# A decoder's router by column tiles, parts shared by a lane's two sequences, and shared experts as threads of their own

## Chip, cores and metric

The kernel runs on one core of a Trainium2 chip. The metric is the time of one execution on the device in microseconds (us). The kernel before has a median of 859.11 us over 13 runs.

## What is computed

Two decoder layers run over x of 16 sequences of 128 tokens with 256 features, in float32. Layer 0 is causal attention with one head, attention to a context of the same size with 16 heads of 16, and a feed-forward part of 16 blocks of which a router keeps four for each token. Layer 1 is self-attention with 16 heads, windowed attention to the context with a rotary embedding, and eight experts of which a router picks two for each token, beside shared experts that all tokens pass. Every part works on the layer norm of x and is added to x:

```python
x = x + _L0_attn_ref(_layernorm(x), qk, ov)
x = x + _L0_xattn_ref(_layernorm(x), ctx, ctx, mask, ...)
x = x + _L0_ffn_ref(_layernorm(x), w_router, b_router, w1, b1, w2, b2)
x = x + _L1_attn_ref(_layernorm(x), w_qkv, b_qkv, w_o, b_o)
x = x + _L1_xattn_ref(_layernorm(x), ctx, ctx, cell, ...)
x = x + _L1_ffn_ref(_layernorm(x), gate_weight, w_gate, w_up, w_down, ws_gate, ws_up, ws_down)
```

The two routers are small products: 256 features to 16 block scores, and 256 features to 8 expert scores, for each token.

## The kernel before

**Lanes.** Eight lanes hold two sequences each (`G = 2`), so a lane is 256 tokens. Its x stays on the chip as `[128 tokens, 2, 256]`. Each part of a layer is a Python generator: it normalises x (`normalise`, line 390: VectorE's bn_stats and bn_aggr, four short GpSimd instructions for `rstd` and `less`, then the two sequences' `xn`, one on VectorE and one on ScalarE), transposes it on TensorE (`tps`, four transposes, copied by ScalarE into `srcT`), and multiplies.

**An attention** (`attention`, for 48 pairs of lane and sequence) takes two passes over the scores. TensorE makes s from `kb` and `qT` in row tiles of 32 (lines with `s<-kb,qT`), sixteen small products add the mask (`s<-unseen,ident`), VectorE takes the maxima (`top`), TensorE transposes them (`topT`), ScalarE and GpSimd put them into the queries (`less`, `qs`), TensorE makes s again (`s<-qs,kb`), ScalarE takes exponentials (`p`), and TensorE multiplies with the values in column tiles of 32 (`oT<-p,v`), transposes (`o`) and hands to VectorE. The score banks (`s`) are two, both taken by one attention at a time.

**Experts.** Lanes 0 to 4 are sorted: `routing` scatters their tokens to DRAM by expert (GpSimd's indirect DMAs), `plan` lays out 27 tiles of 128 rows, and `expert_tile` gathers a tile's weights and rows (`we`), transposes (`xgt`), multiplies (`gu<-we,xgT`), gates, transposes (`hT`), multiplies (`y<-we,hT`) and writes to `by_experts`. `combining` gathers the results back (`yg`, twenty gathers) and adds them to x. Lanes 5 to 7 run all eight experts densely (`expert_ffn`), with `wb` spreading each token's weight. Shared experts of a sorted lane run inside `routing`, as a second thread beside the choice, on the same `srcT`.

**The order of the work** is written when the kernel is built. `Turns` (line 82) is a planner: each generator yields the engine that it wants next and the tiles that it takes, and `run` always resumes the thread with the smallest key: the planned start, then "takes score banks" first, then rank. Costs are planner figures in ns; `SWITCH` is charged when TensorE's tile shape changes, `PART` when TensorE goes to another part, `LEAD` is how far a part that takes score banks may go ahead of its time. `LIMITS` says how many buffers of each kind there are. What the planner decides is then fixed: each engine carries out its own list in order, with semaphores between the engines. `more` starts lanes: five are in flight at once, in the order `TURN`.

**Lines that the steps touch.** `router` (668) makes 16 or 8 scores with the token chunk as the stationary operand and the router's weights moving, two products a sequence; `project` (461) and `values` (488) work one sequence at a time; `causal_attention` (724) runs one thread a sequence; the sums after the feed-forward parts (`y0`, `y1`) are made and added one sequence at a time; lines 134 and 139 are the planner's helpers through which all products and all transposes are recorded, 143 VectorE's, 147 ScalarE's, 153 GpSimd's, 166 the indirect DMAs, 172 and 187 the DMA loads and writes.

Of the kernel before, what the change touches and what calls it, by code (L numbers as in the profile page):

```python
# [54 lines left out]
    ("L1_xattn_b_q", 2), ("L1_xattn_b_k", 2),  # L55
# [3 lines left out]
    ("L1_xattn_b_v", D), ("L1_xattn_b_o", D), ("L0_ffn_b_router", NB),  # L59
# [22 lines left out]
class Turns:  # L82
# [6 lines left out]
    LEAD = 200.0  # L89
# [3 lines left out]
    PART = 40.0  # L93
# [22 lines left out]
    def give(self, tag, n=1):  # L116
        self.tiles[tag] += [self.now.at] * n
# [27 lines left out]
    def act(self, name, out, *args, **kw):  # L145
        self.charge(ACT, 200 + 0.8 * self.width(out, args))
        getattr(self.nc.scalar, name)(out, *args, **kw)  # L147
# [79 lines left out]
    def run(self, more):  # L227

        while True:
            more()  # L230
            best = None
            for i, th in enumerate(self.threads):
                if th.ask is None:
                    continue
                engine, takes = th.ask
                at = self.reach(th, engine)
                ok = True
                for tag, n in takes.items():
                    left = sorted(self.tiles[tag])
                    if not n:  # L240
                        continue
                    if len(left) < n:
                        ok = False
                        break
                    at = max(at, left[n - 1])
                first = "s" in takes
                key = (max(at - self.LEAD * first, self.free_at[engine] - first), not first, th.rank, i)
                if ok and (best is None or key < best[0]):
                    best = key, th, at
# [14 lines left out]
class Thread:  # L264
    def __init__(self, gen, rank, at, parent):
        self.gen, self.rank, self.at, self.parent = gen, rank, at, parent
        self.last, self.ask, self.waits, self.children, self.result = None, None, 0, [], None
# [3 lines left out]
def decoder(ctx: ExitStack, tc: tile.TileContext, a: dict, out: bass.AP):  # L271
# [83 lines left out]
    class Sorted:  # L355
# [3 lines left out]
        def __init__(self, k, lanes):  # L359
            self.lanes, self.left = lanes, len(lanes)  # L360
# [21 lines left out]
        bank=4, s=2, oT=1, xn=5, xT=4, qk=5, qs=2, kb=3, v=3, p=6, oS=2, on=4, xe=3, hm=5, tmp=4,  # L382
        rank=2, selT=2, p0=3, pT0=3, unseen=4, chosen=3, swap=1, words=1, top=3,
# [77 lines left out]
    def project(w, at, xT, j):  # L461

        q.landed(w)
        t = bank([P, D], "pr")
        for d in range(DC):
            q.matmul(t, xT[:, d, j * S : (j + 1) * S], w[:, d, at : at + D], start=d == 0, stop=d == DC - 1)
        return t

# [19 lines left out]
    def values(w, at, xT, bias):  # L488
        yield PE, dict(v=1, bank=1)
        v = v_tiles.pop(0)  # L490
        for j in range(G):
            if j:
                yield PE, dict(bank=1)
            t = project(w, at, xT, j)
            yield DVE
            q.dve(
                "tensor_tensor",
                v[:, j, 0 : H * HA].rearrange("p (h e) -> p h e", e=HA)[:, :, 0:HD],
                t.rearrange("p (h e) -> p h e", e=HD),
                row(bias).rearrange("p (h e) -> p h e", e=HD),  # L500
                ALU.add,
            )
            q.give("bank")
# [29 lines left out]
    def attention(qT, kb, v, j, unseen=None, to=None):  # L533
# [7 lines left out]
        yield PE, dict(s=2)  # L541
        ss = banks()
# [11 lines left out]
        for t2, s in enumerate(ss):  # L554
# [4 lines left out]
            q.give("s")  # L559
        yield PE, dict(bank=1)  # L560
# [16 lines left out]
        yield PE, dict(s=2)  # L577
        ss = banks()
# [12 lines left out]
        def exponentials(s):  # L591
# [3 lines left out]
            q.give("s")  # L595
            return p

        pTs = yield [exponentials(s) for s in ss]
        yield PE, dict(oT=1, bank=1)
# [18 lines left out]
        q.give("bank")  # L618
        yield PE, dict(bank=1)
# [48 lines left out]
    def router(w, xT, n):  # L668
        yield PE, dict(bank=1)
        t = bank([P, G, n], "rt")  # L670
        for j in range(G):
            for d in range(DC):
                q.matmul(t[:, j, :], xT[:, d, j * S : (j + 1) * S], w[:, d, :], start=d == 0, stop=d == DC - 1)
        return t

    def output_projection(on, w, l, j, gain=None, bias=None, free=None):
# [16 lines left out]
        y = project(w, 0, oT, 0)  # L693
# [30 lines left out]
    def causal_attention(l):  # L724
# [8 lines left out]
        def one(j):  # L733
            js = slice(j * S, (j + 1) * S)
            yield PE, dict(bank=1)
            t = project(w["ov"], 0, xT, j)
            yield ACT, dict(on=1)
            v = new("on", [P, D], "v1")
            q.act("copy", v, t)
            q.give("bank")  # L740
            yield PE, dict(bank=1)
            s = bank([P, S], "s0")
            for d in range(DC):
                q.matmul(s, qT[:, d, js], xT[:, d, js], start=d == 0, stop=d == DC - 1)
            yield DVE, dict(p0=1)
            p = new("p0", [P, S], "p0")
            q.dve("tensor_tensor", p, s, causal, ALU.add)
            q.give("bank")
            m = small.tile([P, 1], F32, tag="m0", name="m0")
            q.dve("tensor_reduce", m, p, AX.X, ALU.max, negate=True)  # L750
            yield ACT
            total = small.tile([P, 1], F32, tag="total", name="total")
            q.act("activation", p, p, AF.Exp, bias=m, accum_out=total)
            yield PE, dict(bank=1)
            t = bank([P, S], "pt0")
            q.transpose(t, p, ident)
            q.give("p0")
            yield ACT, dict(pT0=1)
            pT = new("pT0", [P, S], "pT0")
            q.act("copy", pT, t)  # L760
            q.give("bank")
            yield PE, dict(bank=1)
            o = bank([P, D], "o0")
            q.matmul(o, pT, v, start=True, stop=True)
            q.give("pT0")
            q.give("on")
            yield DVE
            r = small.tile([P, 1], F32, tag="r0", name="r0")
            q.dve("reciprocal", r, total)
            q.dve("scalar_tensor_tensor", x[l][:, j, :], o, r, x[l][:, j, :], ALU.mult, ALU.add)  # L770
            q.give("bank")

        yield [one(j) for j in range(G)]
        q.give("xT")
        q.give("qk")

# [32 lines left out]
    def block_ffn(l):  # L809

        xT = yield from transposed((yield from normalise(x[l])))
        rt = yield from router(w["r0"], xT, NB)
        yield DVE, dict(chosen=1)
        pr = small.tile([P, G, NB], F32, tag="pr", name="pr")
        q.dve("tensor_tensor", pr, rt, row("L0_ffn_b_router").unsqueeze(1).to_broadcast([P, G, NB]), ALU.add)
# [15 lines left out]
        for j in range(G):  # L831
            q.pool("tensor_tensor", x[l][:, j, :], x[l][:, j, :], row("L0_ffn_b2"), ALU.add)
# [21 lines left out]
        for j in range(G):  # L854
            yield PE, dict(bank=1)
            y = bank([P, D], "y0")
            for f in range(8):
                q.matmul(
                    y, hm[f // 2][:, f % 2, j * S : (j + 1) * S], w["w2"][:, f, :], start=f == 0, stop=f == 7
                )  # L860
            if j == G - 1:
                q.give("hm", 4)
            yield DVE
            q.dve("tensor_tensor", x[l][:, j, :], x[l][:, j, :], y, ALU.add)
            q.give("bank")

    def self_attention(l):
# [4 lines left out]
        def residual():  # L872
            for j in range(G):

                yield POOL
                q.pool("tensor_tensor", xn[:, j, :], xn[:, j, :], row("L1_attn_b_o"), ALU.add)
                q.pool("tensor_tensor", x[l][:, j, :], x[l][:, j, :], xn[:, j, :], ALU.add)
# [24 lines left out]
    def windowed_attention(l):  # L902
# [31 lines left out]
        def one(j):  # L934
            unseen = yield from by_rows(hidden[1][l * G + j])
            yield from attention(qT, kb, v, j, unseen=unseen, to=on[:, j, :])
            q.give("unseen")
            yield POOL
            q.pool("tensor_tensor", x[l][:, j, :], x[l][:, j, :], row("L1_xattn_b_o"), ALU.add)

        yield [one(j) for j in range(G)]
# [10 lines left out]
    def routing(l):  # L952
# [5 lines left out]
        def choice():  # L958
            rt = yield from router(w["r1"], xT, NE)
            yield ACT  # L960
            sc = small.tile([P, G, NE], F32, tag="sc", name="sc")
            q.act("activation", sc, rt, AF.Exp, scale=-1.0)
            q.give("bank")
# [42 lines left out]
        yield [choice(), shared(l, xT)]  # L1006
        q.give("xT")

    def shared(l, xT):
# [13 lines left out]
        for j in range(G):  # L1023
            yield PE, dict(bank=1)
            y = bank([P, D], "y1")
            for f in range(DC):
                q.matmul(y, hm[:, f, j * S : (j + 1) * S], w["shared"][:, f, 2 * D :], start=f == 0, stop=f == DC - 1)
            if j == G - 1:
                q.give("hm")
            yield DVE  # L1030
            q.dve("tensor_tensor", x[l][:, j, :], x[l][:, j, :], y, ALU.add)
            q.give("bank")
# [198 lines left out]
    def expert_ffn(l):  # L1231

        xT = yield from transposed((yield from normalise(x[l])))
        rt = yield from router(w["r1"], xT, NE)
        yield ACT
        sc = small.tile([P, G, NE], F32, tag="sc", name="sc")
        q.act("activation", sc, rt, AF.Exp, scale=-1.0)
        q.give("bank")
# [47 lines left out]
        for j in range(G):  # L1286
            yield PE, dict(bank=1)
            y = bank([P, D], "y1")
            for f in range(NE + DC):
                down = w["down"][:, f * D : (f + 1) * D] if f < NE else w["shared"][:, f - NE, 2 * D :]  # L1290
                q.matmul(
                    y, hm[f // 2][:, f % 2, j * S : (j + 1) * S], down, start=f == 0, stop=f == NE + DC - 1
                )
            if j == G - 1:
                q.give("hm", 5)
            yield DVE
# [232 lines left out]
```

## Time and profile before

| | us |
|---|---|
| median of 13 runs | 859.11 |
| lowest run | 857.28 |
| the profiled execution, its own time | 857.88 |
| its span, first to last instruction | 856.1 |

| engine | busy us | share of the span |
|---|---|---|
| TensorE, matmuls (PE) | 787.4 | 92% |
| TensorE, weight loads (PEld) | 617.6 | 72% |
| VectorE (DVE) | 471.1 | 55% |
| GpSimd (POOL) | 446.4 | 52% |
| ScalarE (ACT) | 386.5 | 45% |

A product in float32 stands in the trace as two records, a transpose or a bf16 product as one. In a line of the timeline the first number is the start, the second how long the merged records last, and a bracket gives how long the engine sat idle before it and who ended that. Records of TensorE overlap, so the pace of a run of products is read from start to start. PEclk is the clock that TensorE was granted, as a share of full speed.

### The profile page before, as it was taken

How to read it: one execution, taken by the hardware profiler on the slowest of the kernel's cores; microseconds unless marked ns; L12 is line 12 of the kernel's file. 1: busy time of each engine (PE TensorE's matmuls, PEld its weight loads, DVE VectorE, ACT ScalarE, POOL GpSimd, SP SyncE). 2: the span in 40 equal slices, each digit the busy share in tenths (PEclk: the TensorE clock that was granted, in tenths of full speed). 3: DMA queues.
4: the chain of work that ended last, by engine and by line, in shares of the span. 5: the costliest groups of instructions: out<-in, count | busy, mean ns of one | idle time of the engine just before them, and what ended most of it. 6: DMA issues, size and time to landing. Idle time of an engine off the chain costs nothing.

```text
span 856.1 us, 19669 instructions
## 1 busy us (share of the span) xinstructions
PE 787.4 (92%) x7866; PEld 617.6 (72%) x7866; DVE 471.1 (55%) x1232; ACT 386.5 (45%) x864; POOL 446.4 (52%) x700
## 2 busy tenths in 40 slices
PE   6999899999999999999999999899977897989948
PEld 5877578878877777778776777677655575867836
DVE  5535545546544642654767766775784553345534
ACT  4545445343436534364565756346363444343200
POOL 4333636214534534742768759856578654552350
PEclk9999899999999999999999999999998999999988
DMA  8365514410300001001402201001115342452231
GB/s 286 130 179 187 169 42 147 129 26 26 93 27 15 1 2 50 2 3 50 142 32 76 76 14 57 26 26 38 63 63 167 106 136 82 142 159 94 74 105 50
DMA packets 60939, 70.40 MB, mean 82 GB/s; under 512 B 8848, under 2 KB 52496, under 8 KB 60208
## 3 DMA queue, kind: packets, MB, share of 16 engines
q1 hardware_dynamic: 51584, 46.20, 17.0%
q0 software_dynamic: 5376, 19.40, 7.5%
q10 hardware_dynamic: 3888, 3.54, 1.2%
q8 instruction: 62, 1.02, 0.5%
q14 instruction: 29, 0.24, 0.1%
HBM read 43.96 MB, written 20.97 MB: 76 GB/s over the span
## 4 chain that ended last, share of the span: by engine, by line
PE 71%; DVE 9%; POOL 6%; ACT 5%; issue 4%; another core or an unknown queue 2%; DMA 1%; ACTq 0%; DVEq 0%; POOLq 0%
PE s L134 13%; PE y L134 11%; PE pj L134 10%; PE pr L134 9%; PE gu L134 9%; PE hp L134 7%; PE oT L134 4%; PE tps L139 3%; POOL rstd L153 2%; PE o L139 2%; ACT p L147 2%; PE rt L134 1%; DVE top L143 1%; DVE st L143 1%
## 5 line engine op out<-in xcount | busy, mean ns | idle before, releaser
L143 DVE TENSOR_REDUCE top<-s 128x8 f32<-128x1024 f32 x96 | 112.8, 1217 | 57.6 <-PE s L134 50.7
L147 ACT ACTIVATE p<-s 128x1024 f32<-128x1024 f32 x96 | 95.4, 1026 | 52.6 <-PE s L134 43.7
L153 POOL TENSOR_TENSOR qs<-qT,less 128x512 f32<-128x512 f32 x48 | 61.8, 1292 | 89.8 <-ACT less L147 79.8
L134 PE MATMUL hp<-srcT,L_w 128*128 128x256 f32 x256 | 65.9, 387 | 0.6 <-DVE v L143 0.5
L134 PE MATMUL s<-qs,kb 32*128 32x128 f32 x1536 | 59.6, 283 | 7.0 <-POOL qs L153 3.5
L134 PE MATMUL s<-kb,qT 32*128 32x256 f32 x768 | 63.7, 421 | 2.1 <-ACT p L147 2.0
L134 PEld LDWEIGHTS s<-qs,kb 32*128 32x128 f32 x1536 | 49.4, 186 | 21.7 <-issue 8.1
L153 POOL TENSOR_SCALAR rstd<-mv 128x2 f32<-128x2 f32 x72 | 16.5, 229 | 90.4 <-DVE mv L143 66.4
L147 ACT ACTIVATE sg<-gu 128x256 f32<-128x256 f32 (+1 forms) x67 | 22.6, 341 | 90.2 <-PE gu L134 66.7
L134 PE MATMUL gu<-srcT,gu 128*128 128x256 f32 x192 | 51.1, 416 | 9.4 <-DVE hm L143 6.1
L134 PE MATMUL y<-L_w,hm 128*128 128x256 f32 x256 | 58.5, 381 | 0.7 <-DVE x L143 0.7
L153 POOL TENSOR_TENSOR rstd<-rstd,power 128x2 f32<-128x2 f32 x72 | 51.9, 720 | 6.0
L134 PE MATMUL oT<-p,v 128*32 128x128 f32 x1536 | 53.6, 281 | 1.3 <-ACT p L147 1.3
L153 POOL TENSOR_SCALAR kb<-kT,consts 128x256 f32<-128x256 f32 x96 | 53.5, 570 | 1.8 <-ACT kT L147 0.8
L134 PEld LDWEIGHTS gu<-srcT,gu 128*128 128x128 f32 x192 | 38.1, 207 | 21.9 <-DVE hm L143 10.7
L134 PEld LDWEIGHTS y<-L_w,hm 128*128 128x128 f32 x256 | 47.8, 190 | 8.3 <-issue 1.3
L134 PEld LDWEIGHTS hp<-srcT,L_w 128*128 128x128 f32 x256 | 44.5, 190 | 12.1 <-issue 2.9
L134 PEld LDWEIGHTS s<-kb,qT 32*128 32x128 f32 x768 | 39.6, 193 | 18.6 <-issue 9.0
L147 ACT ACTIVATE less<-topT,consts 128x128 f32<-128x128 f32 x96 | 29.6, 372 | 47.1 <-PE topT L139 44.1
L147 ACT COPY oS<-oT 128x512 f32<-128x512 f32 x48 | 28.3, 589 | 46.4 <-PE oT L134 46.1
L134 PEld LDWEIGHTS oT<-p,v 128*32 128x32 f32 x1536 | 40.0, 112 | 12.5 <-issue 8.5
L166 POOL DMA_INDIRECT we<-in_L_experts,tile_weights x27 | 26.6, 984 | 41.6 <-ACT sg L147 14.6
(211 smaller groups left out, 1777.2 us busy)
## 6 DMA issues: line engine op xcount, KB each, us to landing
to_experts<-zero SPq DMA_DIRECT2D x7, 1280.0 KB
unseen<-hidden SPq DMA_DIRECT2D x128, 64.0 KB
c<-in_ctx SPq DMA_DIRECT2D x16, 256.0 KB
by_experts<-we ACTq DMA_DIRECT2D x27, 128.0 KB
x<-in_x SPq DMA_DIRECT2D x8, 256.0 KB
L_w<-in_L_w SPq DMA_DIRECT2D x2, 1024.0 KB
hidden<-plain SPq DMA_DIRECT2D x32, 64.0 KB
swap<-qT SPq DMA_DIRECT2D x16, 128.0 KB
```

What stands on the lines that cost most here:

```text
L134: self.nc.tensor.matmul(out, lhsT, rhs, **kw)
L139: self.nc.tensor.transpose(out, src, ident)
L143: getattr(self.nc.vector, name)(out, *args, **kw)
L147: getattr(self.nc.scalar, name)(out, *args, **kw)
L153: getattr(self.nc.gpsimd, name)(out, *args, **kw)
L166: self.nc.gpsimd.indirect_dma_start(out, at(out_index), src, at(src_index))
```

## The change

It touches the routers, several parts that had been made once for each sequence, the shared experts of the sorted lanes, and the planner.

1. **Router.** The weights are padded to 32 columns and become the stationary operand; four products (two sequences by two feature chunks) write four strips of 32 partitions of one bank `rT`. ScalarE copies it (with the bias of the block router), one transpose brings tokens back to the partitions, and VectorE's reduce adds the two chunks.
2. **A lane's two sequences share parts**: one bank and one copy for the values, one thread of the causal attention for both, one bank and one add for the feed-forward sums (`products`), and one GpSimd add in place of two for biases and residuals.
3. **Shared experts** of lanes 0 to 4 become threads of their own, started when routing ends; they normalise and transpose x again. `combining` starts when all of the group's lanes and the sorted tiles have ended (`part_ended`).
4. **Planner**: `LEAD` 200 to 100, `PART` 40 to 20, a tile given back counts as free 30 ns later (`RELEASE`), ScalarE's operands by row cost 80 ns each, a thread that holds score banks keeps the priority (`holds`), among equals a score or `oT` part goes first while TensorE is in a tiled shape (`tiled`); buffers qs 2 to 3, tmp 4 to 3, p0 and pT0 3 to 2; six lanes in flight in place of five, and layer 1 of lane 0 follows six lanes of layer 0 in place of seven.

```diff
-    LEAD = 200.0
+    LEAD = 100.0
...
-    PART = 40.0
+    PART = 20.0
+    RELEASE = 30.0
...
-        self.tiles[tag] += [self.now.at] * n
+        self.tiles[tag] += [self.now.at + self.RELEASE] * n
...
-                first = "s" in takes
-                key = (max(at - self.LEAD * first, self.free_at[engine] - first), not first, th.rank, i)
+                first = th.holds or "s" in takes
+                tiled = engine == PE and self.shape != WHOLE and ("s" in takes or "oT" in takes)
+                key = (max(at - self.LEAD * first, self.free_at[engine] - first), not first, not tiled, th.rank, i)
...
-        bank=4, s=2, oT=1, xn=5, xT=4, qk=5, qs=2, kb=3, v=3, p=6, oS=2, on=4, xe=3, hm=5, tmp=4,
-        rank=2, selT=2, p0=3, pT0=3, unseen=4, chosen=3, swap=1, words=1, top=3,
+        bank=4, s=2, oT=1, xn=5, xT=4, qk=5, qs=3, kb=3, v=3, p=6, oS=2, on=4, xe=3, hm=5, tmp=3,
+        rank=2, selT=2, p0=2, pT0=2, unseen=4, chosen=3, swap=1, words=1, top=3,
...
-    def router(w, xT, n):
+    def router(w, xT, n, bias=None):
         yield PE, dict(bank=1)
-        t = bank([P, G, n], "rt")
+        t = bank([P, S], "rT")
         for j in range(G):
             for d in range(DC):
-                q.matmul(t[:, j, :], xT[:, d, j * S : (j + 1) * S], w[:, d, :], start=d == 0, stop=d == DC - 1)
-        return t
+                c = j * DC + d
+                q.matmul(
+                    t[c * CT : (c + 1) * CT, :], w[:, d, :], xT[:, d, j * S : (j + 1) * S], start=True, stop=True
+                )
+        yield ACT, dict(p0=1)
+        sb = new("p0", [P, S], "rT")
+        if bias is None:
+            q.act("copy", sb, t)
+        else:
+            q.act("activation", sb, t, AF.Identity, bias=col(bias, 0))
+        q.give("bank")
+        yield PE, dict(bank=1)
+        t = bank([P, G * DC, CT], "rt")
+        q.transpose(t.rearrange("p c n -> p (c n)"), sb, ident)
+        q.give("p0")
+        return t.rearrange("p (g d) n -> p g n d", d=DC)[:, :, 0:n]
...
+    def products(parts):
+
+        y = bank([P, G, D], "y")
+        for j in range(G):
+            pairs = parts(slice(j * S, (j + 1) * S))
+            for i, (a, b) in enumerate(pairs):
+                q.matmul(y[:, j], a, b, start=i == 0, stop=i == len(pairs) - 1)
+        return y
...
-            q.dve("tensor_tensor", p, s, causal, ALU.add)
+        q.dve("tensor_tensor", p, s, causal.unsqueeze(1).to_broadcast([P, G, S]), ALU.add)
...
-        yield [one(j) for j in range(G)]
...
+        for j in range(G):
+            q.act("activation", p[:, j], p[:, j], AF.Exp, bias=m[:, j : j + 1], accum_out=total[:, j : j + 1])
...
-        yield [choice(), shared(l, xT)]
-        q.give("xT")
-
-    def shared(l, xT):
+        yield from choice()
+
+    def shared(l):
+
+        g = group_of[l]
+
+        xT = yield from transposed((yield from normalise(x[l])))
...
+        y = products(lambda js: [(hm[:, f, js], w["shared"][:, f, 2 * D :]) for f in range(DC)])
...
+        part_ended(g)
+
+    def part_ended(g):
+
+        g.parts -= 1
+        if g.parts == 0:
+            at = q.now.at
+            for l in g.lanes:
+                q.start(combining(g, l), 2 * NL + l, at)
...
             g.left -= 1
+            at = q.now.at
+            q.start(shared(l), 2 * NL + l, at)
             if g.left == 0:
-                q.start(sorted_experts(g), 2 * NL + min(g.lanes), q.now.at)
+                q.start(sorted_experts(g), 2 * NL + min(g.lanes), at)
...
-    IN_FLIGHT = 5
+    IN_FLIGHT = 6
...
-    TURN = [(0, l) for l in range(7)]
+    TURN = [(0, l) for l in range(6)]
     for l in range(NL):
-        TURN += [(1, l), (0, l + 7)] if l + 7 < NL else [(1, l)]
+        TURN += [(1, l), (0, l + 6)] if l + 6 < NL else [(1, l)]
```

## The prediction

> **What bounds the kernel now.** I read the page first, then busy time by stretches, then TensorE's timeline, the waits, and last the order in which the instructions of both programs stand on each engine.
>
> ```profile
> span 856.1 us, 19669 instructions
> ...
> PE 787.4 (92%) x7866; PEld 617.6 (72%) x7866; DVE 471.1 (55%) x1232; ACT 386.5 (45%) x864; POOL 446.4 (52%) x700
> ...
> PE   6999899999999999999999999899977897989948
> ...
> PEclk9999899999999999999999999999998999999988
> ```
>
> TensorE is busy 92% of the span and no other engine is over 55%: TensorE is the bound, so a part's cost counts by what it takes on TensorE, and the other engines by how long they leave it idle. The PE row has its low digits in the last quarter. The stretches (us; then busy us of PE, PEld, DVE, ACT, POOL with instructions; granted clock; DMA) put numbers on that:
>
> ```profile
> 8.00:50.00 42.00, 41.02 (x211) 35.14 (x211) 21.78 (x79) 22.38 (x60) 16.58 (x43) 1.00 0.63 209
> 50.00:100.00 50.00, 45.95 (x686) 33.02 (x687) 29.22 (x60) 23.77 (x51) 22.72 (x35) 0.94 0.60 185
> 100.00:640.00 540.00, 517.06 (x5773) 405.48 (x5774) 318.75 (x802) 269.79 (x560) 300.13 (x481) 1.00 0.16 50
> 640.00:806.00 166.00, 146.96 (x1056) 115.20 (x1055) 79.31 (x235) 65.03 (x184) 84.93 (x108) 0.94 0.38 117
> 806.00:834.00 28.00, 17.05 (x69) 13.26 (x68) 9.43 (x23) 2.09 (x6) 17.63 (x19) 0.88 0.41 119
> 834.00:856.00 22.00, 17.94 (x76) 14.76 (x76) 11.03 (x29) 1.54 (x4) 0.00 (x0) 0.90 0.14 48
> ```
>
> From 100 to 640 TensorE is idle 23 of 540 us at full clock: only less work on TensorE shortens it. From 640 on, where the expert tiles run beside the last lanes, it is idle 19.0 of 166 us and the clock is 0.94, so up to 10.0 us more go to the clock (0.06 x 166). From 806 the combining gathers and the last lane's experts leave 11.0 us idle in 28.
>
> **The sum** is made against the profiled execution (857.88 us, span 856.1); the median of the runs shown is 859.11, 1.2 above, which I add at the end. A measurement of this kernel tells about 0.2% (1.7 us) from no change.
>
> **1. Routers.** TensorE's timeline (start, us, then the instructions):
>
> ```profile
> 114.39 1.08 PE L134 MATMUL oT<-p,v 128*32 128x128 f32 x32
> 115.40 1.13 PE L134 MATMUL hp<-srcT,L_w 128*128 128x256 f32 x4
> ...
> 116.48 1.03 PE L134 MATMUL hp<-srcT,L_w 128*128 128x256 f32 x4
> ...
> 117.45 0.96 PE L134 MATMUL rt<-L_router,srcT 128*128 128x16 f32 x8
> 118.27 0.63 PE L139 MATMUL o<-consts,oS 128*128 128x128 f32 x4
> ```
>
> Read from start to start. The old router's 8 records hold TensorE from 117.45 to 118.27, 0.82 us. The new one has the shape of oT (128*32, 128 moving columns), whose 32 records take 1.01 us (114.39 to 115.40): 8 x 0.032 = 0.26 us. Its one transpose costs a quarter of four (0.44 us in rows like o's): 0.11. So 16 routers x (0.82 - 0.26 - 0.11) = -7.2 us. Changing the shape of the array costs 1.13 - 1.03 = 0.10 us; in the orders the changes between whole, row, column and small tiles go from 329 to 333, since the new picking rule sets most routers beside other tiled parts: +0.4 us. If the four column tiles did not run side by side, a router would cost 0.82 + 0.11 + 0.2. The transpose waits for ScalarE's copy (0.28 us, 0.46 with a bias); in the new order 0.4 to 11 us of TensorE's other parts stand between the two (15 of 16 have over 1 us), so behind it on TensorE nothing is held, and the scores come some 0.7 us later to VectorE.
>
> A rule speaks against this step: the Trainium skill, "TensorEngine Tiling (Array Packing)", Instruction Overhead, gives a matmul some 60 cycles however few columns move. By it (an estimate at that section's figure and the 2.4 GHz of "TensorE: Matmul & The Clock Gate") the old router would cost 8 x 0.025 = 0.2 us, and the swap would lose 2.7 us instead of winning 7.2. The row above, 0.10 us per record beside weight loads of 0.2 us mean, decides.
>
> **2. Shared experts as threads.** For five lanes x is normalised and transposed again: 20 transposes x 0.11 = +2.2 us of TensorE. The rest lies on idle engines: VectorE 5 x (2 x 0.407 + 2 x 0.182 + 0.479) = 8.3 us, GpSimd 5 x (0.229 + 0.720 + 0.204 + 0.252) = 7.0, ScalarE 5 x (0.605 + 0.590) = 6.0. GpSimd gets 49.2 us of 256-wide adds back as 32 instructions of 512 (nearest row 1.27 to 1.30 us): 41 us, so it ends 1 us lower. In the most loaded stretch it is 80% busy; without that cover the 7.0 would count. ScalarE also gets 16 router copies (0.28 to 0.46 us each), some 6 us on an engine idle over half the span.
>
> **3. Shared parts.** TensorE's work is the same. VectorE has 24 adds of 512 for 48 of 256 (0.417 each; 512 lies between 0.68, the rank compare, and 0.84, the rotation): between 0 and -3.6 us, hidden. Joined causal attention lengthens a lane's chain by (0.417 - 0.282) + (0.407 - 0.286) + 0.603 + 0.100 + 0.484 = 1.44 us. Other lanes cover it, except at the start: from nothing to 2 x 1.44 = 2.9 us. I take +0.7, because the nearest row, the wait before lane 0's first projection (8.61), is 0.68 and the stretch 8 to 50 has 0.98 idle in all. The last add is 512 wide and waits for both sequences: +0.4 at the end (0 to 0.42).
>
> Work on TensorE: -7.2 + 0.4 + 2.2 = **-4.6 us**; start and end +1.1.
>
> **4. The order.** Six lanes instead of five, LEAD 100, PART 20, RELEASE 30, kept priority for the s parts and qs = 3 cost no instruction; they move parts, and the SP queue carries the same 274 entries. Laid along the orders, the paces above (0.215 us a record of 256 columns, 0.11 a transpose, 1.08 for sixteen s<-kb, 1.10 for thirty-two s<-qs, 0.37 for sixteen masks, 1.02 for oT) add up to 726 us before and 721 after. On that scale the first gathered expert tile stands at 575 and 578, but the last attention's maximum transpose at 618 and 593, the last windowed output at 648 and 621, the last router at 660 and 656. So the last lane's chain from output to router gets 35 us of other work beside it instead of 12, and the five shared pairs move from 362-544 to 452-595. On GpSimd, between the first and the last tile gather, 66 other instructions became 36: two qs instead of four, 4 kb instead of 8, five normalisations instead of seven. What the old order pays there:
>
> ```profile
> 714.38 0.33 PE L139 MATMUL hT<-consts,h 128*128 128x128 f32 x1 [3.13 <-ACT oT L147]
> 715.08 3.63 PE L134 MATMUL pr<-L_xo,oT 128*128 128x256 f32 x8 [0.37 <-ACT oT L147]
> ...
> 766.06 0.29 PE L134 MATMUL ptt<-ident,chosen 128*128 128x128 bf16 x2 [2.87 <-DVE sc L143]
> 766.18 3.63 PE L134 MATMUL gu<-srcT,gu 128*128 128x256 f32 x8
> ```
>
> Each wait of about 3 us is followed by eight records at 3.63 us where they otherwise take 1.89: 1.74 more. With the waits for qs (1.4) and xn (1.4) these chains cost 3.1 + 2.9 + 2 x 1.74 + 2.8 = 12.2 us. The moved parts win between nothing and 12.2 (a new wait of that size in the middle would turn it to a loss, see rival A); half of the layer-1 parts left this stretch and the chain has thrice the cover, so I take two thirds: **-8 us**. Behind these waits gather issues on GpSimd (0.95 us every 1.25) and the by_experts writes on ScalarE's queue. Next late are the xgT copies (4.9 us of waits), which belong to the tiles and stay, as do the 11.0 us from 806 to 834: 20 gathers follow the last tile in both orders.
>
> The Trainium skill, "TensorE: Matmul & The Clock Gate", HAM oscillation, asks for no idle gaps over some 3.4 us. Here gaps of 3.1 and 2.9 us already halve the pace, so a smaller gap costs too; by the rule alone those 3.5 us would not be in the sum.
>
> 857.9 - 4.6 + 1.1 - 8 + 1.2 = 847.6: I forecast **847 us**.
>
> **Rivals.**
> A, slower: the pace of the expert tiles sets the tail. The 27 tiles go from their first row gather at 642.0 to the last tile's copy at 801, 5.9 us each, while a tile needs only 1.6 us of TensorE. If six row buffers, the gathers and the write back hold that pace, less work beside it wins nothing; tiles start 3 us later by the order, and start and end cost 1.1: 859.1 + 3 + 1.1 = 863. It decides once the tiles keep above 5.7 us. For it: GpSimd waits for buffers (14.6 us by sg, 7.9 by by_experts). Against: these are 33 of 166 us, and tiles are picked last, behind lanes that now leave earlier. Chance 0.18.
> B: the order wins nothing, the work alone counts: 859.1 - 4.6 + 1.1 = 855.6. For it: 100 to 640 has little to win. Chance 0.27.
> C, the column tiles run one after another: 16 x 0.31 + 2.2 + 1.1 = +8.3, 867. The oT row speaks against it. Chance 0.03.
> My forecast: 0.52, with 836 to 852 as its own range.
>
> Together: faster 0.52 + 0.22 of B, 0.74; within 0.2% 0.05 (of B); slower 0.21. The range runs from 835 (all 12.2 us won, and some of the 11 after 806) to 863 (rival A's time).
>
> **What would show it.** Right: new routers at 0.25 to 0.3 us from start to start, TensorE's clock from 640 on at 0.96 or more, fewer than 15 us idle in that stretch, no 3 us wait before an output projection or ptt. Wrong: idle from 100 to 640 above 30 us (six lanes crowd the tiles), tiles at 5.9 us each, or a stretch of the gathers longer than the old 28 us.

## The result and the profile after

The changed kernel takes 847.57 us (median of 7 runs, 845.68 to 850.42) where the kernel before takes 859.51 (31 runs): a ratio of 0.987, 95% interval 0.985 to 0.988. The profiled execution took 845.64 us against 857.88. The forecast said 847. The sum came out; half of its terms did not, and most of this part is about that.

The page of the changed kernel (span, busy time, the span in 40 slices, the granted clock):

```profile
span 843.9 us, 19702 instructions
...
PE 775.6 (92%) x7902; PEld 610.5 (72%) x7902; DVE 474.2 (56%) x1201; ACT 393.8 (47%) x874; POOL 446.7 (53%) x688
...
PE   6999999999999999999899899989894899989938
...
PEclk9999999999999999999999999989897899999969
```

TensorE's busy time fell by 11.8 us (787.4 to 775.6) and the rest of the span by 0.4 (68.7 to 68.3). So practically all of the gain is less busy time on TensorE, and the idle time that the forecast wanted to win is still there. The stretches of the changed kernel say where (us; busy us of PE, PEld, DVE, ACT, POOL; granted clock; DMA):

```profile
8.00:50.00 42.00, 41.33 (x242) 35.92 (x243) 21.66 (x72) 21.76 (x54) 17.58 (x46) 1.00 0.63 207
50.00:100.00 50.00, 49.63 (x754) 37.79 (x753) 31.59 (x61) 28.26 (x60) 24.82 (x42) 1.00 0.55 159
100.00:640.00 540.00, 517.03 (x5956) 404.85 (x5954) 324.45 (x781) 283.60 (x586) 309.01 (x474) 0.98 0.17 53
640.00:806.00 166.00, 143.21 (x855) 112.62 (x856) 79.23 (x245) 54.93 (x165) 86.65 (x106) 0.94 0.43 130
```

From 8 to 100 us TensorE was idle 5.0 us and is now idle 1.0. From 100 to 640 nothing changed (22.9 and 23.0). From 640 to 806 it is idle 22.8 us where it was 19.0, at the same clock of 0.94. The timeline of TensorE shows why; the bracket is the wait before the line:

```profile
637.85 0.42 PE L135 MATMUL rT<-srcT,L_router 128*32 128x128 f32 x8
641.17 0.68 PE L140 MATMUL o<-consts,oS 128*128 128x128 f32 x4 [2.90 <-DVE on L144]
641.64 0.42 PE L140 MATMUL rt<-consts,rT 128*128 128x128 f32 x1
647.94 1.38 PE L140 MATMUL ot<-consts,xn 128*128 128x128 f32 x4 [5.87 <-DVE xn L144]
649.14 3.31 PE L135 MATMUL pr<-L_xo,oT 128*128 128x256 f32 x8
...
753.34 0.28 PE L135 MATMUL ptt<-ident,chosen 128*128 128x128 bf16 x2 [2.34 <-DVE chosen L144]
753.46 5.36 PE L135 MATMUL gu<-srcT,gu 128*128 128x256 f32 x16
```

Of the two old waits that of 3.13 us is gone; the one before `ptt` is still there, 2.34 us where it was 2.87. New waits of 2.90 and 5.87 us stand in front of other transposes. The eight records of `pr` take 3.31 us where such a part takes 1.99 at full clock: the clock is at half from 641.6 on for 10.2 us.

### The profile page after: what moved, and what is told of

The parts are those of the page before. It is cut to its first block, busy times and chain, and to the rows that moved or that the text cites. A ratio compares the mean times of both kernels' runs of the same rounds, so it can differ in the third digit from the quotient of the medians.

```text
span 843.9 us, 19702 instructions
## 1 busy us (share of the span) xinstructions
PE 775.6 (92%) x7902; PEld 610.5 (72%) x7902; DVE 474.2 (56%) x1201; ACT 393.8 (47%) x874; POOL 446.7 (53%) x688
## 4 chain that ended last, share of the span: by engine, by line
PE 68%; POOL 12%; DVE 9%; issue 4%; ACT 3%; DMA 2%; another core or an unknown queue 1%; ACTq 0%; POOLq 0%; DVEq 0%
PE s L135 13%; PE pj L135 10%; PE y L135 10%; PE gu L135 9%; PE pr L135 8%; PE hp L135 7%; PE oT L135 4%; PE tps L140 3%; POOL rstd L155 2%; PE o L140 2%; DVE top L144 2%; POOL kb L155 2%; POOL we L168 1%; POOL qs L155 1%
## 5 line engine op out<-in xcount | busy, mean ns | idle before, releaser
L149 ACT ACTIVATE p<-s 128x1024 f32<-128x1024 f32 x96 | 93.2, 1022 | 47.1 <-PE s L135 45.0
L155 POOL TENSOR_SCALAR rstd<-mv 128x2 f32<-128x2 f32 x77 | 18.7, 243 | 105.0 <-DVE mv L144 98.0
L135 PE MATMUL s<-kb,qT 32*128 32x256 f32 x768 | 61.3, 408 | 4.1 <-DVE top L144 2.5
L155 POOL TENSOR_TENSOR rstd<-rstd,power 128x2 f32<-128x2 f32 x77 | 55.8, 724 | 6.4
L155 POOL TENSOR_SCALAR kb<-kT,consts 128x256 f32<-128x256 f32 x96 | 55.2, 586 | 4.6 <-ACT kT L149 3.6
L144 DVE TENSOR_TENSOR x<-x,y 128x512 f32<-128x512 f32 x16 | 11.0, 685 | 76.9 <-PE y L135 76.9
L135 PEld LDWEIGHTS s<-kb,qT 32*128 32x128 f32 x768 | 37.9, 186 | 21.7 <-issue 8.8
L144 DVE SCALAR_TENSOR_TENSOR sg<-sg,gu 128x256 f32<-128x256 f32 (+1 forms) x67 | 24.3, 363 | 44.7 <-ACT sg L149 40.2
L135 PEld LDWEIGHTS gu<-srcT,gu 128*128 128x128 f32 x192 | 37.9, 205 | 15.6 <-DVE hm L144 3.1
```

The source lines that it names most:

```text
L135: self.nc.tensor.matmul(out, lhsT, rhs, **kw)
L144: getattr(self.nc.vector, name)(out, *args, **kw)
L155: getattr(self.nc.gpsimd, name)(out, *args, **kw)
```

## Experiments

The experiments ran in three sets, each on a chip of its own, on which the kernel before takes 842.28, 841.88 and 842.11 us and not the 859.51 of the first comparison. So every experiment is set against these and against the changed kernel's own 827.61 in the second set, whose chip is called the second chip below. The changed kernel ran in that set alone; a difference to it from another set rests on the kernel before taking the same time in all three. "Undone" always means: the changed kernel with one part as it was.

### The same two kernels again

The changed kernel unaltered.

> The changed kernel unaltered. In the first four runs the kernel before took 842.28 us, and 859.51 where the change was first measured, with a granted clock of 0.98 against 0.975. If the change's gain is its own and the two places differ by a common factor, the ratio to the kernel before stays 0.987 (831 us where before takes 842). Rival: the kernel before has two forms of its tail, one 17 us shorter, and the changed kernel keeps its 847: then the ratio is 1.005 and the gain of the first measurement was not the change's alone.

The kernel before unaltered, once more.

> The kernel before, unaltered, for its trace where it takes 842 us. By the common factor every stretch is 2% shorter. By the rival of two forms the stretches up to 640 us agree within 2 us with the first trace, and the 17 us are missing from 640 on: no stall of 8 to 10 us in the gathers' stretch (806 to 834), or no waits of 3 us before hT and ptt.

The changed kernel takes 827.61 us, ratio 0.982 (0.980 to 0.984); the gain is the change's own. The first comparison's kernels are 17 us (before) and 20 us (changed) longer. It is no common factor: in the two traces of the kernel before, TensorE's busy time in the stretches up to 640 us agrees within 0.4 us. The traces show one place for most of the difference. The changed kernel's first trace, while the combining gathers run:

```profile
803.36 1.99 PE L135 MATMUL gu<-srcT,gu 128*128 128x256 f32 x8 [1.45 <-issue]
...
810.55 0.94 POOL L168 DMA_INDIRECT yg<-by_experts,results  x1 [0.30 <-issue]
813.22 0.38 ACT L149 ACTIVATE sg<-gu 128x256 f32<-128x256 f32 x1 [10.82 <-remote]
814.62 0.42 DVE L144 TENSOR_TENSOR hm<-wb,hm 128x256 f32<-128x256 f32 x1 [10.92 <-remote]
...
815.10 0.37 PE L135 MATMUL wb<-selT,experts 128*128 128x256 bf16 x1 [9.74 <-DVE hm L144]
```

ScalarE and VectorE wait for products that TensorE's records show as done, and TensorE then waits 9.74 us for them. In the second trace of the same program there is no such wait. For the kernel before, the same stretch in the trace of the second chip:

```profile
806.00:834.00 28.00, 25.70 (x119) 20.87 (x118) 19.53 (x49) 3.84 (x10) 16.14 (x17) 1.00 0.47 141
```

In the first trace TensorE was busy 17.05 of these 28 us. So the "11.0 us from 806 to 834", which the forecast took for a fixed cost of the end, was mostly this stall.

### One part undone at a time

The routers undone (the old product, its weights unpadded, bias added by VectorE; the functions as in the kernel before):

```diff
-                q.matmul(
-                    t[c * CT : (c + 1) * CT, :], w[:, d, :], xT[:, d, j * S : (j + 1) * S], start=True, stop=True
-                )
+                q.matmul(t[:, j, :], xT[:, d, j * S : (j + 1) * S], w[:, d, :], start=d == 0, stop=d == DC - 1)
```

> The changed kernel with the routers as they were: eight records of 16 (or 8) moving columns on the whole array for each lane and layer, no copy and no transpose; everything else as changed. The forecast's term: 16 x (0.82 - 0.26 - 0.11) = 7.2 us less 0.4 for changes of shape, so this kernel takes 847.6 + 6.8 = 854 us. Rival: the routers' 0.45 us each fall where TensorE waits anyway (its idle time is 64.9 us before and 64.1 after), and the time stays within 2 us of 847.6. In the trace TensorE's busy time should be 7 us above the changed kernel's by either.

850.54 us, ratio to the kernel before 1.010 (1.008 to 1.011): 23 us worse than the changed kernel, and worse than the kernel before, although TensorE's busy time rose by only 10 us (770.4 to 780.5). Neither time that was expected; of the 10 us, 6.1 are the routers' own records.

The planner undone:

```diff
-    LEAD = 100.0
+    LEAD = 200.0
-    PART = 20.0
-    RELEASE = 30.0
+    PART = 40.0
...
-    IN_FLIGHT = 6
+    IN_FLIGHT = 5
```

(with the picking rule, the buffer counts and the order of lanes as before.)

> The changed kernel with the old planner: LEAD 200, PART 40, no RELEASE, no kept priority, the old picking rule, five lanes in flight, the old buffer counts (qs 2, tmp 4, p0 3, pT0 3). The parts' work is as changed. The forecast put 8 us on the order, all of it in the tail: 847.6 + 8 = 856, with the waits of about 3 us before an output projection or ptt back. Rival: the order won nothing there (idle from 640 to 806 went from 19.0 to 22.8 us) and the shared experts as threads alone shortened the tail: within 2 us of 847.6.

858.01 us, ratio 1.019 (1.018 to 1.021): 30 us worse. TensorE is busy 788.1 us, 18 more for the same records, and its clock is at half for 67.8 us (37.8 in the changed kernel). Before its last record it is idle 13 us more (65.1 against 51.9). So more than the 8 us of the forecast went, and not by its waits alone.

The shared experts back inside the routing:

```diff
-        yield from choice()
-
-    def shared(l):
-        xT = yield from transposed((yield from normalise(x[l])))
+        yield [choice(), shared(l, xT)]
+        q.give("xT")
+
+    def shared(l, xT):
```

> The changed kernel with the five lanes' shared experts back inside the routing, on its transposed x, so that a lane's routing ends with them; 20 transposes fewer, all else as changed. By the forecast's sum 2.2 us less work on TensorE, and part of the 8 us of the order given up, since the shared pairs are done before the tail: if half, 847.6 - 2.2 + 4 = 849. Rival 1: the threads are what shortens the tail from the first tile's transposes to the end (207 us before, 190 after): 855 or more. Rival 2: they give nothing and cost their transposes: 845.

852.34 us, ratio 1.012 (1.010 to 1.015): 25 us worse, while TensorE has 3.0 us less to do (767.4 busy). Its chain of waits ends so:

```profile
837.23 0.95 POOL yg L168
838.18 0.30 issue
838.48 2.79 DMA yg<-by_experts,results
...
841.36 0.48 DVE x L144
```

That of the changed kernel on the second chip ends so:

```profile
806.02 2.72 DMA yg<-by_experts,results
...
808.85 0.48 DVE x L144
809.33 0.35 DVE hm L144
...
813.66 8.65 PE y L135 x40
...
822.34 0.69 DVE x L144
```

In the first the end belongs to the gathers of the sorted experts' results; TensorE's last record there ended 28 us before the span did. In the second it belongs to TensorE, and the last gather stands in the chain too: its row's add (`x`) is in VectorE's list just ahead of the gating (`hm`) that TensorE waits for.

The two sequences apart again in the values, the causal attention and the three sums:

```diff
-        t = project(w, at, xT, G)
+        for j in range(G):
+            t = project1(w, at, xT, j)
...
-        y = products(lambda js: [(hm[:, f, js], w["shared"][:, f, 2 * D :]) for f in range(DC)])
+        for j in range(G):
+            y = bank([P, D], "y1")
```

> The changed kernel with a lane's two sequences apart again in the value projections, the causal attention and the three FFN sums (the router, the threads and the order as changed). The forecast priced the joined parts at +1.1 us (start +0.7, end +0.4): 846.5. Rival: the joined parts won, since the stretch 50 to 100 has TensorE busy 49.6 us after against 45.9 before at full clock, a gain that no term had: then 3 to 5 us slower, 851 to 853, with idle time and half clock back between 50 and 104 us.

852.28 us, ratio 1.014 (1.012 to 1.016). From 8 to 100 us TensorE is idle 4.0 us (2.15 up to 50, 1.82 from there) where the changed kernel has 1.0: the rival's idle time, but only 3 of the 25 us, and the half clock is not back (1.00 from 50 to 100). The records of the causal attention take 48.3 us on TensorE where they take 45.3 in the changed kernel.

### The new planner alone

The kernel before with the changed planner and nothing else (the diff above turned round).

> The kernel before with only the new planner: LEAD 100, PART 20, RELEASE 30, kept priority in the attention, the new picking rule, six lanes in flight, qs 3, tmp 3, p0 2, pT0 2. Old routers, shared experts inside the routing, two sequences apart. Forecast: the order is worth 8 us, so 851.5 where the kernel before takes 859.5 (ratio 0.991). Rival: the order wins nothing without the shared experts as threads: ratio 1.000 or more.

856.94 us, ratio 1.017 (1.016 to 1.019): 15 us worse than the kernel before. The rival holds: this order is worth nothing by itself. Four parts, each of which costs 23 to 30 us when it is taken out, and one that costs 15 when it is put in alone: these are not terms of a sum.

### Two ends

What the traces of most of these kernels have in common is a second end. The first two rows are the changed kernel and the kernel before on the second chip; the last four kernels are described below. All columns are us from the span's start.

| kernel | span | PE busy | TensorE's last record ends | last write to by_experts | from that write to the end |
|---|---|---|---|---|---|
| changed | 826.4 | 770.4 | 822.3 | 777.9 | 48.5 |
| before | 841.7 | 783.6 | 837.9 | 799.2 | 42.5 |
| old routers | 849.2 | 780.5 | 834.7 | 810.9 | 38.3 |
| old planner | 857.2 | 788.1 | 853.1 | 814.1 | 43.1 |
| shared inside | 848.0 | 767.4 | 819.8 | 812.0 | 36.0 |
| sequences apart | 850.2 | 772.8 | 836.9 | 812.6 | 37.6 |
| before, new planner | 853.3 | 781.1 | 839.8 | 815.4 | 37.9 |
| old routers, new constants | 835.2 | 775.6 | 819.9 | 797.4 | 37.8 |
| shared inside, new constants | 837.3 | 768.6 | 825.6 | 799.5 | 37.8 |
| before, two constants | 846.7 | 779.8 | 832.5 | 808.8 | 37.9 |
| changed, plan in pieces | 824.1 | 770.7 | 820.0 | 775.5 | 48.6 |

In these traces the span is the later of two ends: TensorE's last record plus 4 us, or the last tile's write plus 36 to 38 us. Four kernels end with TensorE (changed, before, old planner, plan in pieces), seven with the gathers. The second end is made of steps that hardly vary, as two lines of the old routers' trace show (first and last start are the numbers before the semicolon):

```profile
L189 ACTq DMA_DIRECT2D by_experts<-we x27: 326/326/344, 698.9 to 810.9; - x27
L168 POOL DMA_INDIRECT yg<-by_experts,results x20: 940/945/1084, 815.8 to 839.7; - x20
```

From the last write to the first gather 4.9 us, twenty gathers of 0.95 us every 1.25, 23.9 us, and from the last gather to the end 9.5. In the changed kernel the same lines read:

```profile
L189 ACTq DMA_DIRECT2D by_experts<-we x27: 326/326/344, 657.6 to 777.9; - x27
L168 POOL DMA_INDIRECT yg<-by_experts,results x20: 942/946/1030, 782.1 to 806.0; - x20
```

There the tiles are done 33 us earlier, their end at about 777.9 + 38 = 816 is 10 us ahead of TensorE's (826.4), and TensorE's work counts. In the kernel before, 799.2 + 38 = 837 lies 5 us ahead. By this reckoning, had the change brought TensorE's end forward by its 15.6 us and left the tiles at 799, the time would have stopped near 837.

The two ends are not quite apart. In the changed kernel TensorE's last products wait for adds and gatings that stand behind the gathers' adds in VectorE's list:

```profile
795.72 3.72 PE L135 MATMUL gu<-srcT,gu 128*128 128x256 f32 x16 [1.83 <-DVE x L144]
...
800.61 3.72 PE L135 MATMUL gu<-srcT,gu 128*128 128x256 f32 x16 [0.95 <-DVE hm L144]
...
807.25 1.99 PE L135 MATMUL gu<-srcT,gu 128*128 128x256 f32 x8 [0.78 <-DVE hm L144]
...
809.72 1.99 PE L135 MATMUL gu<-srcT,L_shared 128*128 128x256 f32 x8 [0.36 <-DVE hm L144]
```

Together these waits are 3.9 us.

The next three runs test the two ends, and a fourth the waits of 2.90 and 5.87 us.

The old routers, with the planner's constants chosen for that list of parts by the planner's own reckoning of the end (`HOP` and `HOP_FROM_PE` are what it adds when a thread goes from one engine to another):

```diff
-    LEAD = 100.0
+    LEAD = 80.0
-    HOP = 70.0
-    HOP_FROM_PE = 200.0
-    SWITCH = 91.0
-    PART = 20.0
-    RELEASE = 30.0
+    HOP = 60.0
+    HOP_FROM_PE = 220.0
+    SWITCH = 80.0
+    PART = 5.0
+    RELEASE = 40.0
```

> The changed kernel with the old routers, as in the run where that alone cost 23 us, but with the planner's constants chosen anew for it (LEAD 80, PART 5, RELEASE 40, HOP 60, HOP_FROM_PE 220, SWITCH 80, 40 for a per-row operand). Theory: the time is the later of two ends, TensorE's own work and the chain of the expert tiles, which ends some 172 to 178 us after the first tile's weight gather is issued (849.2 - 673.8, 848.0 - 676.2, 850.2 - 672.2 in the runs that undid one part; in the changed kernel that gather is issued at 637.1, and TensorE ends last). With the first tile at 620 to 645 this kernel is bound by TensorE, and the routers cost their 6.8 us: 834 where the changed kernel takes 827.6. Rival: the routers in column tiles are worth the 23 us themselves: 848 or more, whatever the constants.

837.25 us, ratio 0.995 (0.993 to 0.997). The rival falls: at least 13 of the 23 us were the order's. Theory and number agree only in part. TensorE ends at 819.9, no later than in the changed kernel, with 5 us more work; but the tiles end last, at 797.4 + 37.8. The first tile's gather was early (629.0), so the length that I had taken for fixed, 172 to 178 us from there to the end, is not: it is 206 here. What hardly varies is only what follows the last write. Why these tiles go more slowly was not isolated.

The shared experts inside the routing, constants chosen anew:

```diff
-    LEAD = 100.0
+    LEAD = 40.0
-    PART = 20.0
-    RELEASE = 30.0
+    PART = 10.0
+    RELEASE = 15.0
```

> The changed kernel with the shared experts back inside the routing, as in the run where that alone cost 25 us, with the planner's constants chosen anew for it (LEAD 40, PART 10, RELEASE 15). By the theory of two ends, with the first tile's gather before 650 the threads' loss costs nothing but saves the 20 transposes: 825.4 where the changed kernel takes 827.6. Rival: the threads are worth their 25 us by themselves, since they keep work for the tail: 848 or more.

841.17 us, ratio 0.999 (0.998 to 1.000). Both miss: of 25 us, at least 11 were the order's; 14 remain with this one other choice of constants. TensorE ends at 825.6 with the least work in the table but one, and the span ends 11.7 us later with the gathers. Which of its parts held the tiles up was not isolated.

The kernel before with two numbers changed:

```diff
-    LEAD = 200.0
+    LEAD = 100.0
-    PART = 40.0
+    PART = 20.0
```

> The kernel before with two numbers changed and nothing else: LEAD 200 to 100, PART 40 to 20. The forecast gave the whole new order 8 us; the whole new planner put on the kernel before made it 1.7% slower. By the theory of two ends an order fit to the old parts wins some us (835, ratio 0.992) if its first tile's gather stays before 655, and loses if that comes later than 665 (first tile + 178 = 843 or more). Rival: such constants do nothing by themselves, and the gain needs six lanes and the kept priority: within 2 us of 842.

849.38 us, ratio 1.009 (1.007 to 1.011). TensorE's last record comes 5.4 us earlier than in the kernel before (832.5), but the first tile's gather came at 669.1, the last write at 808.8, and the time is 7 us longer. This is the theory's losing branch, which its condition named; that the fixed length behind the condition doesn't hold is shown by the run with the old routers.

The plan of the sorted experts in pieces:

```diff
-        yield DVE, dict(tmp=3)
+        yield DVE, dict(tmp=1)
...
         q.dve("tensor_reduce", tiles, t, AX.X, ALU.add)
+        q.give("tmp")
+        yield DVE
...
+        yield DVE, dict(tmp=1)
         past = new("tmp", [P, T, E1], "past")
```

> The changed kernel with the plan of the sorted experts (22 short VectorE instructions, 634.5 to 640.3 us in its trace, in one piece) cut in six pieces between which other parts may go, on one tmp buffer instead of three; on VectorE only the reciprocal and the scaling of one attention output move ahead, past 12 of them, the rest of the order stays. Theory: the wait of 2.90 us before o<-oS at 638 (634 in the second trace) is the price of standing behind the plan, and some of the 5.5 to 5.9 us wait before ot<-xn that follows, with half clock after both: 824 to 826 where the changed kernel takes 827.6. Rival: the waits move to the next instruction behind the plan: within 1 us.

827.30 us, ratio 0.983 (0.981 to 0.986): the rival. TensorE's timeline shows the wait move:

```profile
634.81 0.66 PE L140 MATMUL o<-consts,oS 128*128 128x128 f32 x4 [0.44 <-ACT oS L149]
635.31 0.27 PE L140 MATMUL rt<-consts,rT 128*128 128x128 f32 x1
644.66 1.37 PE L140 MATMUL ot<-consts,xn 128*128 128x128 f32 x4 [9.08 <-DVE xn L144]
```

2.90 us became 0.44, and the wait behind it, 5.47 in the changed kernel on the second chip, 9.08: the lane's next step, its layer norm, stands behind the rest of the plan (20 instructions; the expectation says 22) on VectorE, and TensorE's list has nothing else to do in between. No version that computes the same result beats the changed kernel by more than the runs scatter.

### The gathers

The combining's twenty row gathers replaced by plain copies of as many bytes (the wrong rows are added):

```diff
-            q.indexed(y[:, i, :], None, g.by_experts, by[:, i : i + 1])
+            nc.sync.dma_start(y[:, i, :], g.by_experts[i * P : (i + 1) * P, :])
```

> The changed kernel, with the 20 row gathers of the combining replaced by plain copies of as many bytes from the same buffer, on SP's queue (so the wrong rows are added); the planner is told the same costs. In the changed kernel's trace TensorE stands still for 9.74 us from 805.36 on, while GpSimd issues these gathers, and gu records that ended by 798 are noticed by ScalarE and VectorE only at 813.2 and 814.6. Theory: the indirect gathers hold up the release of TensorE's results; without them that stall goes and the kernel is 8 to 10 us shorter, 838 to 840. Rival: it is a matter of the order on VectorE or ScalarE, or of the traffic itself: within 2 us of the changed kernel, the stall still there.

821.60 us, 6.0 less than the changed kernel in the same set. It doesn't decide its question: the stall of the first trace is not in the changed kernel's trace of this set either, so there was nothing to remove. It shows that the gathers, with their place in the order, cost some 6 us even where TensorE ends last, by the waits shown above: without them TensorE's last record comes 5.3 us earlier (817.0). The plain copies go out from 765.7 us on, before the last tile is written (778.0), so the 6 us are not the price of the indirect transfer alone. No run made the gathers shorter in a kernel that ends with them.

## Why the prediction was right, and where it was not

**Routers: right.** The forecast read 0.82 us off the old part and priced the new product at 0.26 us and the transpose at 0.11. Five lines of the changed kernel's timeline:

```profile
361.98 1.08 PE L135 MATMUL oT<-p,v 128*32 128x128 f32 x32
362.87 0.40 PE L135 MATMUL rT<-srcT,L_router 128*32 128x128 f32 x8
363.28 0.70 PE L135 MATMUL s<-kb,qT 32*128 32x256 f32 x4
...
365.26 0.33 PE L140 MATMUL rt<-consts,rT 128*128 128x128 f32 x1
365.42 1.03 PE L135 MATMUL hp<-srcT,L_w 128*128 128x256 f32 x4
```

Here the eight records hold TensorE 0.41 us, the transpose 0.16. In the same trace the product takes 0.24 us where `oT`, a part of the same shape, follows, and 0.33 to 0.41 where the shape changes; so 0.26 was right without the shape change, which the forecast had put elsewhere as 0.4 in all. Counting each record until the next one starts or it ends, the sixteen routers took 15.24 us in the kernel before and take 8.28 in the changed one (second chip): 7.0 us less, against 7.2 - 0.4; with the old routers put back they take 6.1 and 6.5 us more than the new. Rival C, column tiles one after another, would have shown 0.8 us for the product. The Trainium skill, "TensorEngine Tiling (Array Packing)", Instruction Overhead, gives each matmul some 60 cycles; the estimate made from that, by which the swap would have lost time, is overruled by these rows.

**Shared experts: the work about right, the worth missed.** 2.2 us were added by the sum; undone, TensorE's busy time falls by 3.0 us, and by 1.8 with the other constants. That without the threads the tiles end later (14 us of time, with constants chosen for their absence) was not in the sum.

**Shared parts: wrong sign.** The forecast had +1.1 us (start +0.7, end +0.4). The start got shorter: of 4 us of idle time that went between 8 and 100 us, the sequences apart bring 3 back. At the end the last add takes 0.69 us for 0.42. And the records of the causal attention (values, scores, transposes, sums) take less time on TensorE for the same products: 2.2 us less in the first pair of traces (47.7 to 45.5), 3.6 on the second chip (49.0 to 45.3, 0.9 of it half clock that only the kernel before has there), and 3.0 more when the sequences are taken apart again. Why the joined records are shorter is open.

**Order: the step that failed.** "Each wait of about 3 us is followed by eight records at 3.63 us ... I take two thirds: -8 us." None of its signs came: idle time from 640 to 806 rose to 22.8 us where fewer than 15 were expected, the clock stayed at 0.94, and waits of 2.90, 5.87 and 2.34 us stand before `o`, `ot` and `ptt`. Of the two chains that were priced, the first is gone (3.13 us and its half clock: `pr` takes 1.93 at 711.75), the second stayed (2.34 us before `ptt`, and half clock behind it), and the 8.8 us of new waits at 638 to 648 took more than was won. The extra cover was real (more parts in the tail), but the plan's 20 short VectorE instructions and one lane's layer norm stand in a row that nothing on TensorE covers. I counted which parts lie between two places of a list, and not when VectorE's list lets the next of them start.

**What made the total come out was luck.** In the first pair of traces, the one that was forecast, the profiled execution falls by 12.2 us: 11.8 of busy time and 0.4 of the rest. Of the busy time 7.0 are the routers and 2.2 the causal attention; 2.6 are spread over the other parts, the 20 added transposes counted in, and no run isolates them. So where the sum had -4.7 (shared experts +2.2, shared parts +1.1, order -8), -5.2 came from terms that it did not hold. On the second chip TensorE's last record comes 15.6 us earlier: 13.1 of busy time (7.0, 3.6 and 2.5) and 2.5 of idle time.

That less work on TensorE shortens the time at all hangs on something the sum did not contain: by the reckoning of two ends the tiles' end lies 5 us ahead of TensorE's in the kernel before and 10 us ahead in the changed one. Rival A named that bound (the tiles' pace sets the tail) and gave it the wrong condition: 5.9 us a tile, where the tiles of the changed kernel, counted in the same way, go at (782.2 - 649.5) / 27 = 4.9. By the table it is the later end in seven kernels, those whose write-to-end is below 39 us. What moves the tiles from one order to the next was not isolated by any run and stays open.

## To carry to other kernels

Where a program picks the order of the work when it is built, a part's price cannot be read from a kernel with that part undone and the same constants: choose the constants again for each list of parts, then compare, and compare busy time beside the time. Look for every chain that could end last, write down how far each is from the end, and treat the gain as capped by the second of them. In the one case tried here, a wait that stood behind a row of short instructions moved to the next instruction behind the row when one was taken past it.

## What the runs showed of the hardware

In the two traces of the first comparison TensorE's results were noticed late while the combining gathers ran: a `gu` product whose last record ended at 798.14 us was taken up by ScalarE at 813.22, and four signals of TensorE came between 813.20 and 814.78, after the last gather had been issued (810.55). In the kernel before, TensorE stood still 5.62 and 3.34 us in the same way. None of the twelve later traces, on three chips, has it, with the same two programs among them. Indirect gathers alone don't bring it about, since eleven of these have them; what does is open.

Four column tiles of 32 run side by side: eight float32 records with 128 moving columns take 0.24 us from start to start, 0.03 us each, the pace of the `oT` parts, where a transpose, a record of 128 columns on the whole array, takes 0.11.

Half clock doesn't need one long wait. In the changed kernel's first trace it comes in stretches of 3.4 us or a multiple, eight of them before TensorE's last record, and in the 3.4 us before each TensorE was idle for 1.1 to 3.4 us in all: 2.34 us ahead of the one at 754.3 (the wait before `ptt`), 1.97 in two pieces ahead of the one at 668.9. Stretches of the same length with 1.4 us of idle time, at 798.6 and 802.0, were not followed by it, so the sum of the idle time alone does not settle it at the low end.
